# Other edge slots in a sparse graph-attention kernel: 70 chunks per pass in place of 72, and another order of blocks and of sorted rows

## The chip, the cores and the metric

The kernel runs on one core of a Trainium2 chip. The metric is device time in microseconds (us) from start to end of one execution. TensorE (PE in the profile, with its weight loads as PEld), VectorE (DVE), ScalarE (ACT), GpSimd (POOL) and SyncE (SP) run their instructions in order, each on its own, and wait for one another with semaphores. Here POOL's queue issues the gathers and SP's queue issues all other transfers.

## The reference

There are 16 graphs of 1024 nodes with 128 features each, and one 1024x1024 adjacency matrix that they all share. Four layers follow one another. L0, L2 and L3 are attention layers with 8 heads of 16 and a feed-forward part, L1 is a graph-attention layer with one head. Every softmax runs over the neighbours of a node alone.

```python
x = 0.0002279 + 0.9999 * normal((16, 1024, 128))
adj = bernoulli(0.0078125, (1024, 1024)).astype(int32)
# L0, L2, L3
scores = einsum('bnhd,bmhd->bhnm', h @ Wq, h @ Wk) / sqrt(16)
scores = where(adj == 0, -inf, scores)
attn_out = einsum('bhnm,bmhd->bnhd', softmax(scores), h @ Wv)
x = layer_norm(h + attn_out @ Wo + bo)
x = layer_norm(x + relu(x @ W1 + b1) @ W2 + b2)
# L1
e = leaky_relu((h @ a_src)[:, :, None] + (h @ a_dst)[:, None, :], 0.2)
y = softmax(where(adj == 0, -inf, e)) @ h + x
```

With the seed of the reference the matrix has 8083 edges, about 8 for each node. A node has at least 1 and at most 17.

## The kernel before

**Sparse work.** The kernel does not form 1024x1024 scores. It writes for each layer a table in DRAM with one row per node: for 8 graphs at once (a group; there are two, `g` = 0 and 1) the keys and values of an attention layer, 8 KB a row, or the transformed features of L1, some 4 KB a row. Then it gathers the row of every neighbour with indirect DMAs.

**Blocks, quarters, chunks.** The nodes are sorted by falling degree. Sorted row `q` is 128 consecutive sorted nodes, and its quarter `j` is 32 of these. Block `t` is made of four quarters from four sorted rows: quarter `j` comes from row `ROWS[j][t]`. `CAPS[t][j]` bounds the degree in that quarter. A *chunk* is one gather of 128 edge slots. A full chunk holds 4 slots of each of the 32 nodes of one quarter. A quarter with cap 10 takes two full chunks, and the two slots left over go to the block's one mixed chunk (`MIX`, lists `QUARTERS` and `SHARED`), which serves what is left of two or three quarters. Slots without an edge get an index out of range, and the bounds check of the gather (L942) leaves their rows out.

**Pieces.** `PIECES` pairs the chunks of a block. A block of 9 chunks has 5 pieces: four pairs, and the mixed chunk alone as the fourth piece. With 11 chunks there are 6 pieces, with 7 there are 4. A *unit* is one block of one layer and group; there are 4 x 2 x 8 = 64, in the order layer, group, block.

**The loop over pieces.** For each piece of an attention unit, `gathered` (L942, POOL) fetches it four pieces ahead into one of four buffers, `products` (L954, DVE) multiplies keys and queries, `exponentials` reduces them (L977, DVE) and takes the exponential (L981, ACT), `weighted` (L1005, DVE) multiplies the values, and `summed` adds them up over the edges on PE: `marked` (L1021) multiplies a 128x32 matrix of ones and zeros (`marks`) with the two halves of the rows, 512 columns each. There is one such matrix for each full chunk, and one for each quarter that a mixed chunk serves. The sums of quarter `j` stand on the partitions 32`j` to 32`j`+31 of the accumulator, so the matmuls of different quarters use different columns of the PE array:

```python
nc.tensor.matmul(
    outs[32 * j : 32 * j + 32], marks[:, mark, :], rhss,
    start=(chunk == mine[0]), stop=(chunk == mine[-1]),
)
```

The first two pieces of a block, with full chunks of four different quarters, are summed together, every other piece by itself. A buffer is free for the next gather when `weighted` is done. In L1 up to four chunks share one part of the loop, and there are no products and no reductions.

**A unit's end and its tail.** `divided` (L1058, L1061) closes a unit in the second piece of the next one: one reciprocal and two multiplications on DVE. It starts two *tails*, the dense remainder of the layer for four graphs each: output projection, norms, feed-forward and the projection into the next layer's table, all on PE and ACT. They run in slices between the pieces of the next unit. `others()`, called three times per piece, hands out slices by `pace`, which divides the steps of a tail by the number of such calls in that unit:

```python
steps -= LATE[units[done][0]]
pace[:] = 0.0, steps / (passes * sum(part[0] == u for part in parts) - 1)
```

When no work of the current unit is waiting, `others()` also advances `slow`: in L0 this is the projection of the second group (`at_leisure`). What is left of it is drained at once before the first gather of that group (`gathered`, `u == T`).

**The setup.** `graph` counts degrees, sorts, and then takes the sorted rows one after the other in the list `order`, which begins with the rows of block 0: fetch the row's part of the matrix (L362, POOL, three rows ahead), mark its edges (L391), and take the largest eight with MAX8 (L396), then the next eight after a MATCH_REPLACE8 (L399), as often as the largest cap of the row asks. Between two rows it yields names, at which the main program does other setup: `load` (the features of block 0), `spread` and `slots` (the indices and marks of block 0) and `queries`. The first gather waits for these indices.

Of the kernel before, what the change touches and what calls it, by code (L numbers as in the profile page):

```python
# [52 lines left out]
J = P // 32  # L53

ROWS = (
    (0, 1, 2, 3, 4, 5, 7, 6),
    (7, 6, 3, 5, 2, 1, 0, 4),
    (7, 6, 5, 1, 2, 0, 3, 4),
    (1, 0, 2, 3, 4, 7, 5, 6),
)  # L60
CAPS = (
    (24, 5, 4, 11), (12, 6, 6, 12), (10, 9, 8, 9), (9, 8, 11, 8),
    (8, 10, 10, 8), (7, 12, 13, 4), (5, 14, 9, 8), (6, 8, 8, 6),
)
TOP = max(map(max, CAPS))
QUADS = TOP // S
MIX = J

# [69 lines left out]
def sparse_path(ctx: ExitStack, tc: tile.TileContext, a: dict, out: bass.AP, flag):  # L138
# [9 lines left out]
    def bank(shape):  # L148
        return banks.tile(shape, F32, tag="ps", name="ps")
# [55 lines left out]

    little = const.tile([P, T * TOP + 32 + 4 * J * QUADS], F32, name="little")
    at = [0]

    def some(*shape, dtype=F32):
        n = at[0]  # L210
        at[0] += int(np.prod(shape))
        t = little[:, n : at[0]]
        t = t if dtype == F32 else t.bitcast(dtype)
        return t.rearrange("p (j k) -> p j k", k=shape[-1])

    lists, mark32 = some(T, TOP), some(1, 32)
    val, used = some(J, QUADS), some(J, QUADS)
# [8 lines left out]
    def graph(wide):  # L226
# [54 lines left out]
        def over_partitions(col):  # L281

            ps = bank([T, P])
            nc.tensor.transpose(ps, col, ident)
            turn = s1.tile([T, P], F32, tag="turn", name="turn")
            nc.vector.tensor_copy(turn, ps)
            dst = accs.tile([P, HF, GH * D], F32, tag="acc", name="acc")
            dst = dst.rearrange("p h d -> p (h d)")
            for t in range(T):
                nc.tensor.matmul(  # L290
                    dst[:, t * P : (t + 1) * P], sel[:, t, :], turn, start=True, stop=True
                )
            return dst
# [39 lines left out]
        for t in range(T):  # L333
# [13 lines left out]
            if t == 0:  # L347
                spread = over_partitions(pack)
# [12 lines left out]
        def by_position(q):  # L361
            return fetch_edges(lambda e: nc.gpsimd.indirect_dma_start(  # L362
                out=e, out_offset=None, in_=a["adj"][:, :],
                in_offset=bass.IndirectOffsetOnAxis(ap=node_i[:, q : q + 1], axis=0),
            ))
# [23 lines left out]
        for at, q in enumerate(order):  # L389
            v = vs[:, :N]  # L390
            nc.vector.scalar_tensor_tensor(v, ahead[at], 0.0, values, ALU.not_equal, ALU.mult)  # L391
            if at + 3 < T:
                ahead.append(by_position(order[at + 3]))
            top = -(-max(SORTED_CAPS[q * J : (q + 1) * J]) // 8) * 8
            for k in range(0, top, 8):
                nc.vector.max(lists[:, q, k : k + 8], v)  # L396
                if k + 8 < top:
                    last, v = v, vs[:, N:] if k % 16 == 0 else vs[:, :N]
                    nc.vector.match_replace(v, lists[:, q, k : k + 8], last, 0.0)  # L399
                yield 1  # L400
            if 0 < at < 5:
                yield ("load", "spread", "queries", "slots")[at - 1]

    def slots():

        def spread(q):
            ps = bank([P, J, TOP])
            for j in range(J):
                nc.tensor.matmul(
                    ps[:, j, :], rep_of(j, True), lists[:, row_of(q, j), :],  # L410
                    start=True, stop=True,
                )
            return ps
# [698 lines left out]
    with tc.manual_schedule():  # L1112
        wide = [gather_buffer() for _ in range(EDGES)]
        setup, entry, weights = graph(wide), at_once(0), load_weights("L0")
        next(setup)
        next(weights)
# [536 lines left out]
```

## The time and the profile before

| | |
|---|---|
| median of 3 runs | 2286.7 us (2286.37 to 2300.34) |
| span of the profiled execution | 2290.8 us |
| PE busy | 2052.0 us |
| DVE busy | 1871.1 us |
| ACT busy | 1530.3 us |
| POOL busy | 1050.7 us |
| gathers (L942) | 576, in 8 passes of 72 |
| moved | 636.06 MB, of which 485.08 MB by POOL's queue |

A pass is one layer and group, eight units. The first product on DVE begins at 101.2 us, the last reciprocal at 2252.9 us. Between one reciprocal (L1058) and the next lies the same kind of work in every attention unit: one closing, the pieces 2 and later of one unit and the first two of the next, and two tails. The prediction reads the profile in such *intervals*.

In a row of groups, the columns are the line, the engine, the operation, output and inputs with their shape and the count, then the busy time in us and the mean in ns, then the idle time of the engine ahead of it and what ended most of that. In a row of windows they are the stretch and its length, and for each engine its busy time in that stretch and how many instructions that was.

### The profile page before, as it was taken

What the parts mean: (1) busy time and instruction counts of PE and PEld (TensorE: products, weight loads), DVE (VectorE), ACT (ScalarE), POOL (GpSimd) and SP (SyncE); (2) the same over time, 40 slices, a digit from 0 to 9 for tenths busy, and PEclk for the clock granted to TensorE, in tenths of its full rate; (3) what the DMA queues carried; (4) which work ended last, traced back from release to release, by engine and by line L of the source; (5) the groups of instructions that cost most, each with busy time, mean ns of one, the idle gap of its engine ahead of it and who ended that gap; (6) DMA issues with size and microseconds to landing.
All of it is one profiled execution on the core that took longest, in us unless ns stands there. A gap on an engine that the chain in (4) does not pass through costs nothing. (4 is left out here: it accounts for less than half of the span.)

```text
span 2290.8 us, 36572 instructions
## 1 busy us (share of the span) xinstructions
PE 2052.0 (90%) x13140; PEld 1271.6 (56%) x13140; DVE 1871.1 (82%) x1472; ACT 1530.3 (67%) x5041; POOL 1050.7 (46%) x730
## 2 busy tenths in 40 slices
PE   6479999899998999998899989999999988998987
PEld 5336666555555555554465655655655555555544
DVE  7898888588888477777988889988888887988783
ACT  3237777777776565556677777777777766776765
POOL 3355344245445278884443434333344444444540
PEclk8789999999999999999999999999999998999999
DMA  7868888678887699997998978888887877677750
GB/s 249 278 217 300 304 279 305 240 247 302 285 295 265 197 330 354 354 373 288 326 318 292 319 254 306 296 314 295 281 282 277 291 258 250 242 275 270 260 217 20
DMA packets 165197, 636.06 MB, mean 278 GB/s; under 512 B 35064, under 2 KB 37880, under 8 KB 116510
## 3 DMA queue, kind: packets, MB, share of 16 engines
q0 software_dynamic: 89216, 485.08, 59.3%
q1 hardware_dynamic: 75792, 148.57, 18.9%
q8 instruction: 105, 1.72, 0.3%
q14 instruction: 84, 0.69, 0.1%
HBM read 581.08 MB, written 92.34 MB: 294 GB/s over the span
## 5 line engine op out<-in xcount | busy, mean ns | idle before, releaser
L942 POOL DMA_INDIRECT e<-table,idx x576 | 844.2, 1466 | 1022.1 <-DVE pr L1005 796.6
L1005 DVE TENSOR_TENSOR pr<-e,ex 128x2048 f32<-128x2048 f32 (+1 forms) x320 | 661.3, 2075 | 55.9 <-ACT ex L981 32.7
L954 DVE TENSOR_TENSOR pr<-e,qr 128x2048 f32<-128x2048 f32 x192 | 439.7, 2290 | 160.3 <-DMA e<-table,idx 91.5
L1021 PE MATMUL acc<-pr,marks 128*32 128x512 f32 x2624 | 528.5, 616 | 20.3 <-DVE pr L1005 16.4
L977 DVE TENSOR_REDUCE sc<-pr 128x128 f32<-128x2048 f32 (+1 forms) x240 | 497.5, 2073 | 8.0
L620 ACT ACTIVATE z<-yps,root 128x128 f32<-128x128 f32 x888 | 319.0, 390 | 35.6 <-PE yps L735 16.8
L1021 PEld LDWEIGHTS acc<-pr,marks 128*32 128x32 f32 x2624 | 108.7, 111 | 280.9 <-issue 231.6
L635 ACT ACTIVATE z<-yps,rstd 128x128 f32<-128x128 f32 x888 | 255.0, 371 | 7.2
L731 PE MATMUL yps<-W,f 128*128 128x128 f32 x1520 | 252.6, 283 | 7.7 <-ACT f L726 1.9
L726 ACT ACTIVATE f<-ps,b 128x512 f32<-128x512 f32 x190 | 130.6, 695 | 160.4 <-PE ps L717 159.7
L731 PEld LDWEIGHTS yps<-W,f 128*128 128x128 f32 x1520 | 205.7, 193 | 51.7 <-issue 26.2
L572 PE MATMUL ps<-Wkv,xT 128*128 128x256 f32 x768 | 212.2, 417 | 20.0 <-ACT xT L648 14.4
L908 ACT COPY qr<-ps 128x512 f32<-128x512 f32 x384 | 197.1, 602 | 47.7 <-PE ps L905 47.7
L642 PE MATMUL ps<-ident,z 128*128 128x128 f32 x896 | 179.7, 300 | 41.4 <-ACT z L635 36.6
L642 PEld LDWEIGHTS ps<-ident,z 128*128 128x128 f32 x896 | 116.2, 143 | 167.7 <-ACT z L635 86.5
L717 PE MATMUL ps<-x,W 128*128 128x512 f32 x384 | 193.9, 630 | 12.5 <-ACT x L650 12.4
L620 ACT ACTIVATION_READ_ACCUMULATOR z<-yps,root 128x1 f32 x888 | 203.7, 229 | 0.0
L905 PE MATMUL ps<-q,rep 32*128 32x512 f32 x768 | 166.5, 661 | 36.4 <-ACT q L900 34.0
L572 PEld LDWEIGHTS ps<-Wkv,xT 128*128 128x128 f32 x768 | 146.5, 204 | 73.9 <-ACT qr L908 18.0
L981 ACT ACTIVATE ex<-sc 128x128 f32<-128x128 f32 (+1 forms) x240 | 76.4, 318 | 157.9 <-DVE sc L977 157.8
L576 ACT COPY kv<-ps 128x512 f32<-128x512 f32 x176 | 103.3, 593 | 108.1 <-PE ps L572 85.8
L706 PE MATMUL yps<-Wo,oT 128*128 128x128 f32 x768 | 159.9, 291 | 10.0 <-ACT oT L648 10.0
(174 smaller groups left out, 2724.2 us busy)
## 6 DMA issues: line engine op xcount, KB each, us to landing
table<-kv SPq DMA_DIRECT2D x88, 512.0 KB
kept<-xT SPq DMA_DIRECT2D x96, 256.0 KB
x<-kept SPq DMA_DIRECT2D x48, 512.0 KB
qx<-qr SPq DMA_DIRECT2D x48, 256.0 KB
e<-table,idx POOLq DMA_INDIRECT x576
table<-kv SPq DMA_DIRECT2D x32, 256.0 KB
qx<-qr SPq DMA_DIRECT2D x18, 384.0 KB
qx<-qr SPq DMA_DIRECT2D x42, 128.0 KB
```

Of the source, the lines that this page charges most:

```text
L572: nc.tensor.matmul(ps[:, k, :], x[:, i + k, :], w[LAYERS[l][0], "Wkv"], start=True, stop=True,)
L620: nc.scalar.activation(z[:, i, :], y[:, i, :], AF.Square, scale=D**-0.5, bias=root, accum_out=total[:, i : i + 1],)
L635: nc.scalar.activation(z[:, i, :], y[:, i, :], AF.Copy, scale=rstd[:, i : i + 1])
L642: nc.tensor.transpose(ps[:, i, :], z[:, i, :], ident)
L717: nc.tensor.matmul(ps, p["W1"][:, f * P : (f + 1) * P], x1.rearrange("p g n -> p (g n)"), start=True, stop=True,)
L731: nc.tensor.matmul(ps[:, i, :], f1[:, f, i * P : (i + 1) * P], p["W2"][:, f, :], start=(f == 0), stop=False,)
L908: nc.scalar.copy(qs[u][:, j, h * GH * D : (h + 1) * GH * D], pss[j])
L942: nc.gpsimd.indirect_dma_start(out=es[i][:, k, :], out_offset=None, in_=tables[l, g][:, :], in_offset=bass.IndirectOffsetOnAxis(ap=idx[:, ...
L954: nc.vector.tensor_tensor(prs[i][0][:, :n, :], es[i][:, :n, :ROW], qx[u].rearrange("p (o c) -> p o c", o=1) if (MIX, 0) in piece else of_p ...
L977: nc.vector.tensor_reduce(sc[:, :n, :], prs[i][0][:, :n, :].rearrange("p k (a d) -> p k a d", d=HD), mybir.AxisListType.X, ALU.add,)
L1005: nc.vector.tensor_tensor(prs[i][k0 // 2][:, :m, :].rearrange("p k (a d) -> p k a d", d=d), es[i][:, k0 : k0 + m, base : base + ROW].rearr ...
L1021: nc.tensor.matmul(outs[32 * j : 32 * j + 32], marks[:, mark, :], rhss, start=(chunk == mine[0]), stop=(chunk == mine[-1]),)
```

## The change

The two lists are other ones, the largest cap falls from 24 to 22 (`TOP` is rounded up to the same 24), and the places at which `graph` yields are moved by one row, with `slots` ahead of `queries`.

```diff
 ROWS = (
-    (0, 1, 2, 3, 4, 5, 7, 6),
-    (7, 6, 3, 5, 2, 1, 0, 4),
-    (7, 6, 5, 1, 2, 0, 3, 4),
-    (1, 0, 2, 3, 4, 7, 5, 6),
+    (2, 3, 0, 4, 5, 6, 7, 1),
+    (2, 1, 6, 3, 0, 4, 5, 7),
+    (3, 4, 7, 2, 5, 0, 1, 6),
+    (3, 4, 7, 1, 5, 2, 0, 6),
 )
 CAPS = (
-    (24, 5, 4, 11), (12, 6, 6, 12), (10, 9, 8, 9), (9, 8, 11, 8),
-    (8, 10, 10, 8), (7, 12, 13, 4), (5, 14, 9, 8), (6, 8, 8, 6),
+    (10, 10, 8, 8), (9, 11, 8, 8), (22, 6, 4, 4), (8, 9, 9, 10),
+    (8, 14, 8, 6), (6, 8, 13, 9), (5, 8, 11, 12), (12, 5, 6, 5),
 )
-TOP = max(map(max, CAPS))
+TOP = -(-max(map(max, CAPS)) // 8) * 8
@@ graph()
-            if 0 < at < 5:
-                yield ("load", "spread", "queries", "slots")[at - 1]
+            if at < 4:
+                yield ("load", "spread", "slots", "queries")[at]
```

What follows from the lists, by the rules above, and from the reference's degrees:

| block | chunks, before | after | pairs of two chunks of one quarter, before | after | quarters of the mixed chunk, before | after | edges, before | after |
|---|---|---|---|---|---|---|---|---|
| 0 | 11 | 9 | 2 | 0 | 2 | 2 | 1037 | 1115 |
| 1 | 9 | 9 | 0 | 0 | 2 | 2 | 1034 | 1068 |
| 2 | 9 | 9 | 0 | 2 | 3 | 2 | 1051 | 830 |
| 3 | 9 | 9 | 0 | 0 | 2 | 3 | 1072 | 1120 |
| 4 | 9 | 9 | 0 | 1 | 2 | 2 | 1056 | 1030 |
| 5 | 9 | 9 | 0 | 0 | 2 | 3 | 1021 | 1092 |
| 6 | 9 | 9 | 0 | 1 | 3 | 2 | 1008 | 1028 |
| 7 | 7 | 7 | 0 | 1 | 2 | 3 | 804 | 800 |
| all | 72 | 70 | 2 | 5 | 18 | 19 | 8083 | 8083 |

So only block 0 loses chunks: its sixth piece. That piece was chunks 4 and 5 of the quarter with cap 24, and it held 2 edges in 256 slots. The list `order` is 0, 1, 7, 2, 3, 4, 5, 6 before and 2, 3, 0, 1, 4, 5, 6, 7 after.

## The prediction

> **What bounds the kernel now.** I read the busy time of the engines first, then the costliest groups, then windows of one interval each (from one reciprocal L1058 to the next), then single instructions there. The chain of waits ends after four entries and carries nothing.
>
> ```profile
> PE 2052.0 (90%) x13140; PEld 1271.6 (56%) x13140; DVE 1871.1 (82%) x1472; ACT 1530.3 (67%) x5041; POOL 1050.7 (46%) x730
> ...
> L1005 DVE TENSOR_TENSOR pr<-e,ex 128x2048 f32<-128x2048 f32 (+1 forms) x320 | 661.3, 2075 | 55.9 <-ACT ex L981 32.7
> L954 DVE TENSOR_TENSOR pr<-e,qr 128x2048 f32<-128x2048 f32 x192 | 439.7, 2290 | 160.3 <-DMA e<-table,idx 91.5
> ...
> L977 DVE TENSOR_REDUCE sc<-pr 128x128 f32<-128x2048 f32 (+1 forms) x240 | 497.5, 2073 | 8.0
> ```
>
> Two engines are close to full, so the averages decide nothing. A full pair costs DVE three instructions of some 2.29 us, 6.8 us. The windows show one pass of L3 (six pieces of block 0, then five pieces of block 1, then six five-piece intervals together) and six five-piece intervals of each L2 pass:
>
> ```profile
> 1654.60:1696.00 41.40, 37.84 (x232) 21.82 (x231) 39.00 (x21) 28.42 (x92) 16.88 (x10) 1.00 0.79 275
> 1696.00:1733.00 37.00, 35.48 (x239) 23.14 (x240) 32.31 (x19) 29.08 (x92) 13.11 (x10) 1.00 0.89 314
> ...
> 1105.00:1324.60 219.60, 208.81 (x1339) 132.90 (x1338) 194.93 (x117) 165.64 (x529) 88.30 (x60) 0.97 0.87 306
> 1400.80:1619.90 219.10, 208.71 (x1344) 132.42 (x1344) 193.28 (x108) 165.74 (x531) 84.49 (x60) 0.98 0.89 309
> 1696.00:1919.90 223.90, 203.59 (x1312) 123.77 (x1312) 192.75 (x109) 161.63 (x522) 100.34 (x70) 0.97 0.77 279
> ```
>
> After stretch and length come PE, PEld, DVE, ACT, POOL, then the PE clock, the DMA share and GB/s. With six pieces DVE is the fuller engine (39.0 of 41.4 us, PE 37.8). With five it is PE: 95% in L2, 91% in L3, DVE 86 to 89%. What DVE waits for in a five-piece unit of L2:
>
> ```profile
> 1562.63 2.36 DVE L954 TENSOR_TENSOR pr<-e,qr 128x2048 f32<-128x2048 f32 x1 [1.74 <-PE acc L1021]
> ...
> 1571.76 2.29 DVE L954 TENSOR_TENSOR pr<-e,qr 128x2048 f32<-128x2048 f32 x1 [3.31 <-PE ps L717]
> ```
>
> PE is the releaser both times. So DVE bounds block 0, PE the other blocks. In L3, POOL's output scatters wait for the tails and hold back the gathers queued behind them: 20.6 us of DVE's waits for gathered rows lie in 1682 to 1906, and PE sets part of those.
>
> How PE's edge sums are priced decides the rest. These three runs of L1021 stand in block 0 of L3: four full chunks of four quarters, a pair of two quarters, a pair of one quarter.
>
> ```profile
> 1667.99 1.92 PE L1021 MATMUL acc<-pr,marks 128*32 128x512 f32 x16
> 1671.83 1.91 PE L1021 MATMUL acc<-pr,marks 128*32 128x512 f32 x8
> ...
> 1687.48 3.62 PE L1021 MATMUL acc<-pr,marks 128*32 128x512 f32 x8
> ```
>
> Sixteen matmuls on four column groups take what eight take on two. Eight on one column group take 3.62 us. A **same-quarter pair** costs PE 3.62 - 1.91 = 1.71 us more, one *step*. A mixed chunk of three quarters costs none: its 12 matmuls took 1.92 us.
>
> [...]
>
> **The change part by part.**
>
> *The sixth piece of block 0 goes* in six attention passes: 6.8 us of DVE, and on PE the 3.62 us of its sum and one step in the other same-quarter pair, 5.3 us. What remains is a five-piece interval, so I take the difference between the six-piece interval and its next neighbour: L0 second group 44.5 - 37.6 = 6.9, L2 41.4 - 37.3 = 4.1, L3 41.4 - 37.0 = 4.4 and 40.6 - 37.4 = 3.2. In L2's first pass DVE was busy for 38.5 of 39.1 us, after a light tail of L1: 6.0 of its 6.8. Sum -24.6 us. In the very first unit (DVE 40.8 of 43.9 us, PE 21.4) all of 6.8 is gained: **-31.4 us**.
>
> *Less room for the second group's projection.* Its idle calls in block 0 shrink with the pieces. By the instruction order 4 transposes and 4 kv matmuls move to the drain ahead of that group's first gather, where POOL waited 27.9 us for the table. Eight L572 records take 2.0 us, four transposes 0.6: **+2.6 us**.
>
> *Same-quarter pairs elsewhere.* Block 0 had two, now blocks 2, 4, 6 and 7 have 2, 1, 1 and 1: 5 steps, 8.6 us of PE per attention pass. What hides them is PE's idle time, 1.7 to 3.9 us an interval, much of it waits for ACT that stay. DVE's slack does not hide them, since DVE already waits for PE. I count them in full in L0's first pass (PE 155.4 of 166.5 us, and its block 7 lies in the drain), at 0.9 in L0's second and both of L2, at 0.75 in L3, where the scatters give slack: 8.6 x (1 + 2.7 + 1.5) = **+44.7 us**. Ends: 0.3 of 6 x 8.6 = 15 us, and all, 52.
>
> *L1.* Up to two pieces are summed together there, and a part is as long as its fullest quarter (20 records with two matmuls deep in one took 3.63 us). A pass goes from 32 to 34 steps, +3.4 us of PE: 3 fewer in block 0, 5 more elsewhere. PE is 99% busy there (102.33 of 103.3 us in the second group) and so are the DMA engines. Both passes +6.8 if PE decides, 0 if the transfers do; I take **+4 us**.
>
> *The setup.* The row sizes, hence DVE's 13 MAX8 and 5 MATCH_REPLACE8 (1.23 us each), are the same, so extraction ends at the same time. Only the queue order moves. Before, the first gather went at 89.37, released by block 0's indices. They are now ready after rows 2, 3 and 0: 61.5 + 5.0 + 5.0 + 7.7 + 3.9 = 83.1. But POOL's last row fetch waits for L391 of the fifth row, behind row 1: 83.1 + 5.0 + 1.2 = 89.3. That fetch and one of features follow (2 x 1.25), and the gather starts near 92.0: **+2.6 us**. Ends: -1, if the tables land sooner, and +5. The earlier `load` puts its two fetches (L852, 0.95 us each) ahead of the fifth row fetch on POOL, and their transposes on PE wait less for rows (6.3 us before). `queries` follows `slots`, which has nothing more on PE, so PE's order there stays: the queries' last copy ended at 92.3, the first product began at 101.2. SP's copies move with them.
>
> *At nothing:* bytes (the bounds check leaves empty slots out, and 8083 edges give the same 485 MB), POOL's 16 fewer gathers (1.47 us each, beside 1022 us idle), one more qx copy a pass on SP, the smaller `ex`. The fuller blocks 0, 1, 3 and 5 gather up to 8% more; at a DMA share of 0.72 to 0.89 I hide it.
>
> Sum: -31.4 + 2.6 + 44.7 + 4 + 2.6 = +22.5 us on the profiled span of 2290.8. Those 2290.8 us stand 4.1 above the median; I put the difference on the median: **2309 us**, 1.0% slower.
>
> **The rivals.**
>
> *Half hidden.* The steps fit into PE's idle time at 0.5: 26 in place of 44.7, L1 +2: 2286.7 + 2 = 2288. For it: a block with one step more than 1.71 us idle could swallow it. Against: block 2 gets two, and L2 idles only 1.7.
>
> *DVE decides, faster.* If PE catches up wherever DVE has work, DVE's saving stands: 6 x 6.8, one L1005 of 2.3 in each L1 pass, less 2.6, 42.8 us, so 2244. For it: DVE was full with six pieces, while PE kept up with two same-quarter pairs. Against: DVE's waits above. The sign turns once the steps count below some 0.4 (22 us of 52); 2244 needs them at nothing.
>
> *The gathers decide.* The four fuller blocks carry 4395 edges, 214 more than four times the 1045 that blocks 0 to 5 had on average: 1.75 MB, at 348 GB/s (289 at a DMA share of 0.83 in L0's second group) 5 us a pass. If a third lands on DVE: 10 more, 2319. Against: blocks 2 and 7 carry fewer.
>
> *The change doesn't do what it says.* If a degree exceeded the new caps, the dense program would follow. The largest degrees of the sorted quarters are 17, 14, 12, 12, 11, all within 22, 14, 13, 12, 12 and so on down, so I give it nothing.
>
> **How the numbers follow.** PE decides, at 0.75 to 1: 0.55, around 2309 (2300 to 2320). Half hidden: 0.27 (2278 to 2300). DVE decides: 0.08. Gathers on top: 0.10 (2316 to 2335). The range 2284 to 2325 leaves out the DVE case, the low end of the half-hidden one and half of the gathers. About 1%, 22.9 us, is what a measurement can tell here: slower takes over half of the first case and the gathers, 0.42; faster is the DVE case, 0.08; 0.50 lies between.
>
> **What would show it.** Six-piece intervals of 41 us become 37. Intervals with block 2 lengthen by about 3 us, those with blocks 4, 6 and 7 by 1 to 1.7, with PE as the releaser of L954 or L1058; L1021 shows runs of 3.62 us there. The first gather starts near 92. I am wrong if block 2's intervals stay at 36 to 38, or if DVE's waits name DMA instead.

## The result

The changed kernel takes 2302.2 us (median, 2293.8 to 2311.2), the kernel before on the same chip 2291.1. The ratio is 1.0052, with an interval of 1.0031 to 1.0073: 7 to 17 us slower. All ratios below are to runs of the kernel before on the same chip, because its median moved between 2285 and 2301 us from one set of runs to the next. One of 22 executions of a later kernel (more room for side work) took 3966.6 us and is left out of its ratio. The profiled execution took 2304.1 us with a span of 2302.3, against 2290.8 before. These are the engines and the costliest groups of the changed kernel:

```profile
PE 2066.0 (90%) x13092; PEld 1275.6 (55%) x13092; DVE 1828.8 (79%) x1452; ACT 1526.4 (66%) x5035; POOL 1011.4 (44%) x714
...
L1005 DVE TENSOR_TENSOR pr<-e,ex 128x2048 f32<-128x2048 f32 (+1 forms) x312 | 642.9, 2069 | 75.5 <-ACT ex L981 35.6
L1021 PE MATMUL acc<-pr,marks 128*32 128x512 f32 x2592 | 558.0, 618 | 21.7 <-DVE pr L1005 20.3
L954 DVE TENSOR_TENSOR pr<-e,qr 128x2048 f32<-128x2048 f32 x186 | 425.4, 2287 | 173.0 <-DMA e<-table,idx 90.1
L977 DVE TENSOR_REDUCE sc<-pr 128x128 f32<-128x2048 f32 (+1 forms) x234 | 483.7, 2067 | 7.8
```

DVE lost 42.3 us of work, as the removed instructions say. PE got fuller by 14.0 us although it issues 48 matmuls fewer. The wait in front of L1005 rose from 55.9 to 75.5 us. So DVE's saving was spent on waiting, and the question is where.

I cut both executions at the reciprocals that close block 7, which gives one length per pass (layer and group). In us:

| pass | before | after | difference | in the interval of block 0 |
|---|---|---|---|---|
| start to first product | 101.2 | 105.6 | +4.4 | |
| L0, first group | 355.4 | 378.5 | +23.1 | -0.4 |
| L0, second group | 299.3 | 300.8 | +1.5 | -4.8 |
| L1, first | 159.0 | 163.7 | +4.7 | -4.7 |
| L1, second | 150.9 | 148.5 | -2.4 | -6.0 |
| L2, first | 293.5 | 290.9 | -2.6 | -5.1 |
| L2, second | 295.2 | 292.3 | -2.9 | -4.5 |
| L3, first | 302.1 | 294.6 | -7.5 | -4.5 |
| L3, second | 296.1 | 289.2 | -6.9 | -4.3 |

One pass loses 23 us, and the seven others together gain 16. Each length is that of one execution: between kernels of this study that have the same instructions in a pass, its length differed by up to 5.7 us, so a single small difference here says little. Of the 4.4 us ahead of the first product, 3.4 were there before the change acts: the degrees were counted at 58.4 instead of 55.0. In five kernels with the setup of before the first product began at 99.0 to 103.0 us, in four with the changed one at 101.4 to 105.6.

The removed sixth piece shows where it was expected. Windows of the changed kernel, blocks 0 and 1 in the first pass of L3, where six pieces had taken 41.40 us:

```profile
1680.24:1717.16 36.92, 35.44 (x233) 22.86 (x233) 32.30 (x18) 29.13 (x95) 13.22 (x8) 1.00 0.96 324
1717.16:1753.06 35.90, 33.96 (x229) 21.78 (x228) 32.21 (x19) 28.50 (x90) 13.12 (x10) 1.00 0.85 294
```

In the first pass it does not show. First its block 0, block 1 and the drain of the second group's projection in the kernel before, then the same three stretches in the changed kernel:

```profile
101.23:162.49 61.26, 34.16 (x151) 14.06 (x151) 57.66 (x76) 10.98 (x25) 29.11 (x17) 0.72 0.68 248
162.49:203.23 40.74, 37.84 (x252) 24.82 (x252) 35.82 (x39) 30.66 (x99) 17.80 (x12) 1.00 0.77 274
...
410.64:456.67 46.03, 39.87 (x246) 27.15 (x246) 25.75 (x15) 30.76 (x98) 15.65 (x12) 0.93 0.64 229
```

```profile
105.58:166.44 60.86, 27.34 (x124) 12.52 (x124) 51.13 (x75) 9.80 (x22) 22.23 (x15) 0.61 0.66 245
166.44:215.58 49.14, 42.55 (x254) 26.41 (x254) 35.72 (x40) 30.44 (x100) 20.93 (x13) 0.87 0.65 225
...
431.12:484.08 52.96, 44.10 (x263) 29.05 (x264) 25.76 (x16) 32.60 (x101) 14.98 (x12) 0.94 0.62 225
```

In block 0 DVE works 6.5 us less (57.66 to 51.13), and the stretch is only 0.4 us shorter. The difference is waiting. The first product of block 1 on DVE's timeline, in the changed kernel and then in the one before:

```profile
149.11 2.29 DVE L954 TENSOR_TENSOR pr<-e,qr 128x2048 f32<-128x2048 f32 x1 [6.47 <-ACT qr L908]
```

```profile
145.18 2.29 DVE L954 TENSOR_TENSOR pr<-e,qr 128x2048 f32<-128x2048 f32 x1 [1.45 <-ACT qr L908]
```

It waits for the queries of block 1. They belong to the front work that `others()` does between the pieces. Five pieces make 15 calls of it, six made 18. What is left at the end of the unit is done in one go, and DVE stands by.

This gives two theories for the loss: the room for side work in the first pass, or the same-quarter pairs, as predicted. Both could be tried alone.

### The profile page after: what moved, and what is told of

It reads as the page before. It is cut to its first block, busy times and chain, and to the rows that moved or that the text cites. A ratio compares the mean times of both kernels' runs of the same rounds, so it can differ in the third digit from the quotient of the medians.

```text
span 2302.3 us, 36411 instructions
## 1 busy us (share of the span) xinstructions
PE 2066.0 (90%) x13092; PEld 1275.6 (55%) x13092; DVE 1828.8 (79%) x1452; ACT 1526.4 (66%) x5035; POOL 1011.4 (44%) x714
## 5 line engine op out<-in xcount | busy, mean ns | idle before, releaser
L942 POOL DMA_INDIRECT e<-table,idx x560 | 819.7, 1464 | 1072.0 <-DVE pr L1005 834.3
L1005 DVE TENSOR_TENSOR pr<-e,ex 128x2048 f32<-128x2048 f32 (+1 forms) x312 | 642.9, 2069 | 75.5 <-ACT ex L981 35.6
L1021 PE MATMUL acc<-pr,marks 128*32 128x512 f32 x2592 | 558.0, 618 | 21.7 <-DVE pr L1005 20.3
L954 DVE TENSOR_TENSOR pr<-e,qr 128x2048 f32<-128x2048 f32 x186 | 425.4, 2287 | 173.0 <-DMA e<-table,idx 90.1
L977 DVE TENSOR_REDUCE sc<-pr 128x128 f32<-128x2048 f32 (+1 forms) x234 | 483.7, 2067 | 7.8
L1021 PEld LDWEIGHTS acc<-pr,marks 128*32 128x32 f32 x2592 | 116.6, 111 | 306.1 <-issue 259.8
L572 PE MATMUL ps<-Wkv,xT 128*128 128x256 f32 x768 | 207.3, 409 | 34.3 <-ACT xT L648 28.2
L642 PE MATMUL ps<-ident,z 128*128 128x128 f32 x896 | 177.8, 299 | 37.5 <-ACT z L635 32.6
L642 PEld LDWEIGHTS ps<-ident,z 128*128 128x128 f32 x896 | 115.7, 143 | 158.4 <-ACT z L635 80.3
L572 PEld LDWEIGHTS ps<-Wkv,xT 128*128 128x128 f32 x768 | 142.6, 199 | 85.6 <-ACT xT L648 31.8
L905 PE MATMUL ps<-q,rep 32*128 32x512 f32 x768 | 160.8, 642 | 29.0 <-ACT q L900 27.6
```

Source lines behind the costliest of these rows:

```text
L572: nc.tensor.matmul(ps[:, k, :], x[:, i + k, :], w[LAYERS[l][0], "Wkv"], start=True, stop=True,)
L642: nc.tensor.transpose(ps[:, i, :], z[:, i, :], ident)
L942: nc.gpsimd.indirect_dma_start(out=es[i][:, k, :], out_offset=None, in_=tables[l, g][:, :], in_offset=bass.IndirectOffsetOnAxis(ap=idx[:, ...
L954: nc.vector.tensor_tensor(prs[i][0][:, :n, :], es[i][:, :n, :ROW], qx[u].rearrange("p (o c) -> p o c", o=1) if (MIX, 0) in piece else of_p ...
L977: nc.vector.tensor_reduce(sc[:, :n, :], prs[i][0][:, :n, :].rearrange("p k (a d) -> p k a d", d=HD), mybir.AxisListType.X, ALU.add,)
L1005: nc.vector.tensor_tensor(prs[i][k0 // 2][:, :m, :].rearrange("p k (a d) -> p k a d", d=d), es[i][:, k0 : k0 + m, base : base + ROW].rearr ...
```

## The experiments

### The pairs alone, put on the kernel before

```diff
+PIECES[1][2], PIECES[1][4] = [(0, 1), (0, 2)], [(3, 1), (3, 2)]
+PIECES[5][2], PIECES[5][4] = [(1, 1), (1, 2)], [(2, 1), (2, 2)]
+PIECES[6][2], PIECES[6][4] = [(1, 1), (1, 2)], [(2, 1), (3, 1)]
```

> The kernel before with its own lists, but the last chunks of blocks 1, 5 and 6 paired within one quarter: 5 more same-quarter pairs, 5 x 1.71 = 8.6 us more of PE in each attention pass, and nothing else changed on DVE or in the transfers. Theory (PE's idle time and block 0's DVE-bound intervals hide most steps): the six passes of L0, L2 and L3 lengthen by 0 to 3 us each, L2 and L3 least; in all +5 to +18 us on the kernel before. Rival (the steps count nearly in full, as predicted): each of the passes lengthens by 6 to 9 us, in all +40 to +55 us.

Ratio 1.0155 (1.012 to 1.0189): +36 us, closer to the rival than to the theory. By pass, against before: L0 +10.3 and +7.3, L1 +5.1 and +7.0, L2 +2.9 and +6.7, L3 -2.6 and +4.6. The attention passes make 29.2 of 51.6 us, a share of 0.57 in this one execution. L1 pays 12.1 of its 13.7 (four pairs a pass are deep there). So the pairs are expensive, but unevenly: in full in L0 and nearly so in L1, hardly at all in the first groups of L2 and L3.

### Two of the pairs taken from the changed kernel

```diff
+PIECES[4][2], PIECES[4][4] = [(0, 1), (1, 1)], [(1, 2), (2, 1)]
+PIECES[6][2], PIECES[6][4] = [(1, 1), (3, 1)], [(2, 1), (3, 2)]
```

> The changed kernel with the pairs of blocks 4 and 6 mixed over quarters: 2 of its 5 new same-quarter pairs go, 3.4 us of PE in each attention pass. Theory (steps mostly hidden): 0 to 8 us less than the changed kernel, so 2294 to 2303 where it has 2302. Rival (steps nearly in full): 2/5 of 44.7 and a little of L1, 18 to 20 us less, so about 2283; L2's and L3's intervals of blocks 4 and 6 each 1.3 to 1.7 us shorter.

Ratio 0.9995 (0.9978 to 1.0013), against 1.0052 of the change as it is: some 13 us less, between the two. The pairs of blocks 2 and 7 cannot be mended this way, since one quarter holds all that is left to pair there.

### More room for side work in the first unit of the changed kernel

```diff
             others()
+            if i < 3:
+                others()
             if 0 < i <= len(parts):
```

> The changed kernel with one more call of the side work in each of the first three pieces, 18 calls in the first unit as before (it had 15). Theory (the first pass lost 23 us because the front work of the first units and the second group's projection no longer fit): the first pass comes back by 10 to 20 us, most of it in the first two intervals and in the drain, and the time is 2282 to 2292. Rival (the first pass is longer for its same-quarter pairs and its fuller blocks): the first pass stays within 4 us of the changed kernel's 378.5, and the time at about 2302.

Ratio 1.0002 (0.9985 to 1.0019), 11 us less than the change as it is. The first pass fell from 378.5 to 365.9 us: 4.2 in the interval of block 0, 3.1 in that of block 1, 5.3 in the drain. The theory holds for about half of the 23 us. The rest is pairs (alone they put +10.3 on this pass) and a difference between executions that the next run shows, less what block 0 gains.

### Less room in the kernel before

```diff
-            others()
+            if i != 5:
+                others()
```

(at its three places in the loop)

> The kernel before without the three calls of the side work in the sixth piece of its first unit: 15 calls there as in the changed kernel, with the six pieces kept. Theory: the first pass (355 us) lengthens by 8 to 20 us, most of it in the intervals after the first and in the drain, and the time goes to 2297 to 2310. Rival: the first pass stays within 4 us, and so does the time.

Ratio 1.0018 (1.0003 to 1.0034), +4 us: short of what the theory asked. (Its 2300.4 us lie in the stated range, but the kernel before took 2294.2 on that chip.) The first pass is 9.3 us longer in the profile, 3.9 in the drain and 5.9 in block 1. In block 1 PE stands still for 3.47 us ahead of L572, and that comes with the calls: all four kernels with 15 of them have this gap, 3.47 or 3.48 us (the changed one, the one with two pairs less, this one, and the sixth piece alone below), and in the nine with 18 or 20 no gap of PE within this interval is over 0.92 us. What it costs cannot be read from the 5.9 us, though. A later run whose first pass has the same instructions as the kernel before (the one without output writes, below) is as slow in block 1:

```profile
163.64:209.68 46.04, 43.14 (x263) 29.64 (x264) 35.64 (x39) 31.32 (x101) 19.24 (x13) 0.88 0.72 247
```

The kernel before took 40.74 us there with the TensorE clock at 1.00, this one 46.04 at 0.88: it ran at half clock for 13.65 us around the start of block 1, after PE had stood still for 4.47 us at the end of block 0. Of the nine kernels with 18 or 20 calls, six spend 10 to 14 us of block 1 or its start at half clock and take 45.0 to 48.6 us for it. So some 5 of the 23 us in the table above are a difference between executions, and the profile of the kernel before is one of the lucky ones. What is left for the calls is the drain, +3.9, which agrees with the time.

### The sixth piece alone, without and with the room

The largest degrees in block 0's quarters are within 17, 5, 4 and 10. With these bounds it has nine chunks and five pieces, and one same-quarter pair instead of two.

```diff
-    (24, 5, 4, 11), (12, 6, 6, 12), (10, 9, 8, 9), (9, 8, 11, 8),
+    (17, 5, 4, 10), (12, 6, 6, 12), (10, 9, 8, 9), (9, 8, 11, 8),
...
-TOP = max(map(max, CAPS))
+TOP = 24
```

> The kernel before with only block 0's bounds closer (17, 5, 4, 10 in place of 24, 5, 4, 11): its sixth piece and one same-quarter pair go, every other block, all rows and the order stay. Theory (the sixth piece was priced rightly, the first pass was not): 4 to 5.5 us less in the first interval of each pass after the first, 7 x 4.7 = 33 us, and in the first pass a loss of 0 to 9 us for the three calls of side work that go with the piece (their loss alone gave +9.3 in the kernel before): 20 to 32 us less than before, 2262 to 2274. Rival (the prediction as it stood: the first unit gains 6.8 as well, the drain loses 2.6): the first pass 4 us shorter, the first unit's interval 6 to 7 us shorter.

> The kernel before with block 0's closer bounds as in the run above, and one more call of the side work in each of the first three pieces. Theory: the first pass comes back by 6 to 12 us against the run without the calls, the rest of the passes is alike, the time is 2254 to 2264, the shortest of all kernels. Rival (calls packed into fewer pieces crowd PE and ACT, so that nothing comes back): within 3 us of the run without the calls.

Without further calls the ratio is 0.9905 (0.9882 to 0.9928), some 22 us less than before. With the three calls it is 0.9835 (0.9815 to 0.9856), 38 us less, the best ratio in the study. Block 0 and the drain of the first pass with the calls:

```profile
103.85:157.99 54.14, 27.17 (x135) 12.08 (x133) 51.05 (x74) 10.25 (x23) 22.71 (x15) 0.72 0.79 279
...
414.03:457.88 43.85, 36.94 (x246) 25.58 (x246) 25.67 (x15) 30.49 (x98) 16.09 (x12) 1.00 0.64 232
```

DVE is busy for 51 us in block 0 as in the changed kernel, but the stretch takes 54.14 us instead of 60.86. Without the calls it took 63.18, and the drain 49.95; block 1 took the same to 0.1 us. Both theories stand: the first unit does gain about its 6.8 us (7.1 measured), if the side work keeps its calls. In the changed kernel with the three calls it gained 4.6.

### L3 without the output writes, without and with the pairs

Why do the pairs cost so little in L3? DVE's waits in its first pass, in the kernel before (in all, times, longest):

```profile
DVE pr L954 <- DMA e<-table,idx: 31.0, 7, 5.9
DVE pr L954 <- PE acc L1021: 5.8, 3, 3.4
DVE both L1058 <- PE ps L1021: 3.3, 2, 3.2
```

DVE waits three times as long for gathered rows as for PE. If that is what covers the pairs, they must show once the waits go.

```diff
+        if (l, g, t) != units[-1]:
+            return
         nc.gpsimd.indirect_dma_start(
             out=out.rearrange("n (k c) -> (n k) c", k=GR * HF),
```

> The kernel before without the writes of the output, all units but the last: 30 of its 32 output scatters on POOL's queue are left out, and nothing else. It is the base for the next run. Theory (in L3 the scatters wait for the tails and hold back the gathers behind them): DVE's waits for gathered rows in the two passes of L3, 31.0 and 31.8 us before, fall below 12 each, and the passes, 302 and 296 us before, shorten by 8 to 20 us each. Rival (the gathers are late for other reasons): the waits stay above 20.

> The run above (the output writes left out but for the last unit) with the 5 more same-quarter pairs of the first experiment in blocks 1, 5 and 6. Theory (in L3 the waits for gathered rows covered the pairs): without the scatters each pass of L3 lengthens by 5 to 9 us for its 8.6 us of pairs, where it changed by -2.6 and +4.6 with them. Rival (the pairs are hidden by something else in L3, a rising TensorE clock or ACT's waits): the passes of L3 change by less than 4 us each.

The scatters do hold the gathers back. The same view without them:

```profile
DVE pr L956 <- DMA e<-table,idx: 14.3, 6, 3.3
DVE pr L956 <- PE acc L1023: 6.0, 3, 3.4
```

The two passes of L3 shorten by 10.6 and 12.9 us, the ratio is 0.9905 (0.9877 to 0.9933). In the second pass the waits are down to 8.5 us; the 14.3 of the first are more than the 12 expected. But with the pairs added L3 changed by +0.3 and +4.5, about as little as with the scatters in place, where 5 to 9 were expected: the theory fell. It is not refuted for the first pass altogether, since 14.3 us of late gathers were left there and 9.5 with the pairs.

The other passes repeat the first experiment (L0 +11.0 and +7.5, L1 +7.1 and +6.4, L2 -0.3 and +6.5), so the pattern is not the accident of one profile. Its level is less sure. The profiled execution with pairs was the slowest of 18: its span is 42 us longer than without, where the medians differ by 26. And of the +10.3 and +11.0 in L0's first pass 3.9 and 5.4 lie in the intervals of blocks 0 and 1, where executions differ by some 5 us.

What takes the pairs up in L3's first pass is idle time of PE. First without pairs, then with them:

```profile
1659.82:1951.34 291.52, 269.88 (x1727) 165.26 (x1726) 258.88 (x144) 213.43 (x694) 119.40 (x80) 0.97 0.76 271
...
1697.68:1989.49 291.81, 275.22 (x1727) 166.46 (x1726) 258.80 (x145) 214.01 (x694) 118.34 (x80) 0.98 0.76 271
```

PE works 5.3 us more in a pass that is only 0.3 us longer. The waits of its transposes (L642 in the kernel before) for ACT fell from 10.7 to 5.6 us, and from 17.0 to 12.9 in the first experiment. In the second pass they fell from 12.4 to 9.3, and from 21.2 to 18.0.

In the first pass of L2 it is something else. Its groups of PE, without pairs, then with them:

```profile
L1023 PE MATMUL acc<-pr,marks 128*32 128x512 f32 x328 | 68.5, 619 | 6.9 <-DVE pr L1007 6.9
...
L572 PE MATMUL ps<-Wkv,xT 128*128 128x256 f32 x127 | 36.7, 426 | 1.4 <-ACT qr L910 0.6 <-ACT kv L576 0.5 <-issue 0.2
L719 PE MATMUL ps<-x,W 128*128 128x512 f32 x56 | 28.9, 640 | 1.7 <-ACT x L650 1.7
```

```profile
L1026 PE MATMUL acc<-pr,marks 128*32 128x512 f32 x328 | 76.1, 611 | 6.3 <-DVE pr L1010 6.3
...
L575 PE MATMUL ps<-Wkv,xT 128*128 128x256 f32 x127 | 34.4, 405 | 2.1 <-ACT qr L913 2.1
L722 PE MATMUL ps<-x,W 128*128 128x512 f32 x56 | 27.1, 606 | 1.7 <-ACT x L653 1.7
```

The edge sums take 7.6 us more, near the 8.6 that the pairs ask. The same matmuls of the projection and of the feed-forward part, as many as before, take less: 426 to 405 ns and 640 to 606. PE's busy time in the pass is 270.73 us without and 270.89 with pairs, and its mean granted clock rose from 0.95 to 0.98 (from 0.95 to 0.97 in the first experiment, where PE's busy time rose by 2.0 us). In L2's second pass the clock fell from 0.98 to 0.97, and there the pairs cost 6.5 us. Over all thirteen kernels the clock of L2's first pass is 0.965 to 0.982 in the six with pairs in the later blocks and 0.941 to 0.976 in the seven without. The clock was not set by itself in any run, so this is a reading with its numbers; why PE's waits shrink in one pass and its clock rises in another stays open.

### Both mends, and two more tries

The changed kernel with the mended pairs and the three calls:

> The changed kernel with both mends: the pairs of blocks 4 and 6 mixed over quarters, and one more call of the side work in each of the first three pieces. Theory (two separate causes): the gains add, 12 and 9 us, so 20 us less than the changed kernel and 0.5% less than the kernel before (ratio 0.992 to 0.997). Rival (both only shorten the same drain of the first pass): no better than the better of the two, ratio 0.998 to 1.001.

Ratio 0.9931 (0.9908 to 0.9953), 1.2% less than the change as it is. The gains add, as separate causes would (20 us were expected, it is some 28, and the intervals leave room for either).

On the sixth piece alone with its calls (the best version), the condition `i < 3` became `here and u == 0`, 20 calls:

> The kernel before with block 0's closer bounds (five pieces), with one more call of the side work in each of the first unit's five pieces: 20 calls instead of 18. Theory (18 calls restore the room that the kernel before had, more brings the second group's projection further ahead of the drain at the price of the first two units): within 4 us of the run with 18 calls, whose ratio to the kernel before was 0.9835. Rival (the room is still the limit of the first pass): 5 to 9 us less, the drain interval of the first pass 2 to 4 us shorter and the second unit's interval 3 to 6.

Ratio 0.9859 (0.983 to 0.9888), which overlaps the interval of the run with 18 calls. The first pass is the same to 0.2 us: 18 calls are enough, as the theory said.

And the scatters two steps of the tail later (`for _ in range(4): yield` in place of two yields in `finish`):

> The kernel before with block 0's closer bounds and 18 calls, and with the output scatters issued two steps of the tail later. Theory (a scatter that waits on POOL's queue for its rows holds the gathers back): DVE's waits for gathered rows in L3's two passes, some 31 us each, fall below 20, the two passes shorten by 5 to 12 us each, the ratio to the kernel before goes from 0.9835 to 0.973 to 0.979. Rival (the later scatters pile up before the end of each unit and hold the gathers there): L3's passes stay within 4 us, the ratio at 0.982 to 0.986.

Ratio 0.9859 (0.9831 to 0.9888); the waits for gathered rows are 34.2 and 31.9 us (34.6 and 28.7 without the shift), L3's passes within 1.2 us. The theory fell: issuing them later does not help, only leaving them out did.

## Why the prediction was right, and where it was not

The time lay 7 us under the forecast and inside its range, with the sign right. Part of that is luck. Of the forecast difference of 22.5 us some 12 came, and the kernel before took 2291.1 us in this comparison where the forecast started from 2286.7. Two of its terms were mis-sized, in opposite directions.

| term | predicted | measured |
|---|---|---|
| sixth piece, five later attention passes | -24.6 | -23.2 (table above) |
| sixth piece, the very first unit | -6.8 | -0.4; with the calls kept -4.6 in the changed kernel, -7.1 with the sixth piece alone |
| less room for the projection | +2.6 | 11 us for the room as a whole (time), 12.6 (profile) |
| pairs in the attention passes | +44.7 | 29.2 and 29.5 for five pairs (profiles); less by the medians |
| L1 | +4 | +2.3 |
| setup | +2.6 | +0.9 from the counted degrees to the first product, not told from noise |

**The sixth piece** was priced from neighbouring intervals, and that method held within 1.5 us for the sum of five passes (single ones were off by up to 2.1). That DVE bounded block 0 agrees with this, but no run shows it by itself: with the piece, PE lost work too.

**The first unit** failed at "all of 6.8 is gained". I argued from DVE's busy share there. But the number of calls follows from the number of pieces, and I counted the lost calls only for what they push into the drain, at 2.6. The same calls also make block 1's queries, and DVE waited 5 us longer for these. Keeping the calls gave back 4.2 us in this interval, 3.1 in the next and 5.3 in the drain, 11 to 13 us in all.

PE's timeline in block 1 of the changed kernel shows the form that the loss takes:

```profile
183.17 0.60 PE L642 MATMUL ps<-ident,xg 128*128 128x128 f32 x4
187.25 2.08 PE L572 MATMUL ps<-Wkv,xT 128*128 128x256 f32 x4 [3.48 <-ACT xT L648]
189.25 3.57 PE L1021 MATMUL acc<-pr,marks 128*32 128x512 f32 x8
...
203.29 1.03 PE L572 MATMUL ps<-Wkv,xT 128*128 128x256 f32 x4
204.25 1.91 PE L1021 MATMUL acc<-pr,marks 128*32 128x512 f32 x8
```

The projection now stands right behind its own transposes and waits 3.48 us for ACT to copy them. Around that gap PE runs at half clock: the granted clock was 0.50 from 185.8 to 192.6 us and 1.00 on both sides; the same four matmuls took 2.08 us there and 1.03 later, the eight edge sums 3.57 and 1.91. That the gap brings the half clock on was not shown: in the four kernels with this gap the clock record falls between 1.4 us ahead of its end and 1.5 us behind it, and each of them has a second stretch of half clock, 3.41 us, near the end of the interval, where no gap is over 1.14 us.

**The pairs** failed at their shares: 1.0 in L0's first pass, 0.9 in its second and L2, 0.75 in L3. Measured, as the mean of the two experiments over 8.6 us: 1.24 and 0.86 in L0, 0.15 and 0.77 in L2, -0.13 and 0.53 in L3. The price of one pair held (7.6 us of edge sums for an expected 8.6). The step that failed is "What hides them is PE's idle time [...] much of it waits for ACT that stay. DVE's slack does not hide them, since DVE already waits for PE". The waits for ACT did not stay: in L3's first pass those of the transposes fell by 5.1 and 4.1 us when pairs were added. And a wait for PE shows that PE's end decides, but not that more matmuls make that end later. In the changed kernel block 2 has two such pairs, and its interval lengthened by 3.7 and 2.8 us in L0 but changed by -0.7, +1.3, -0.4 and -1.7 in L2 and L3. With 35.7 to 37.9 us it stayed there at the 36 to 38 which the prediction named as a sign of being wrong.

**The rivals.** "Half hidden" had the share about right (0.57 in the profiles, 0.5 assumed), but not its time of 2288, which has the first pass as the forecast had it. "DVE decides" is out: with the pairs alone the kernel became 1.55% slower. "The gathers decide" is out: DVE's waits for gathered rows were 13.2 us in L2 and 62.8 in L3 before, and are 16.6 and 60.8 after.

Put the measured terms in place of the predicted ones (-23.2, -7.1, 11 to 12.6, 29.4, 2.3, 0.9), and the 22.5 us become 13 to 15, inside the measured 7 to 17. This is no close test: the medians of the two pair experiments, +36 and +26 us, leave 24 and 13 for the attention passes if L1 takes what the profiles show, and with these the sum is -3 to 9.5. The forecast came near because the pairs were put at least 15 us too high and the lost room 8 to 10 too low.

## What to carry to other kernels

When a loop iteration is removed, list what rides on its slots: side work that is sliced by iteration loses its room, and what it feeds is late far from the edit. Three further calls were worth 11 to 16 us here, where the piece without them was worth 22. And price added matmuls by an experiment in each kind of pass: the same 8.6 us cost 7.4 us in L0's second pass and 1.3 in L2's first (profiles of two experiments), though DVE waited for PE in both.

## What was not expected of the hardware

In one pass, more work on TensorE hardly made it busier: with 7.6 us more of edge sums in the first pass of L2, PE's busy time went from 270.7 to 270.9 us at a clock of 0.98 in place of 0.95. And block 1 of the first pass, the same program in both, took 40.74 us in one execution and 46.04 in another (252 and 263 matmuls fell into it), at a clock of 1.00 and 0.88: ahead of the second, PE had stood still for 4.47 us, and in the last 9 us ahead of the first for no longer than 1.26 us at a time. Three calls fewer, on the other hand, put a gap of 3.47 to 3.48 us of PE into every kernel that had them, and half clock near it. What sets the clock was not shown.
